# A four-layer transformer in one launch: bias, mask and weight rows change engines in four of its stages

## The chip, the cores and the metric

The kernel runs on one core of one Trainium2 chip. The metric is the time of one execution on the device, in microseconds (us); lower is better. A core has five engines that each work through a queue of their own in order: TensorE (PE, matrix products; its weight loads are PEld), VectorE (DVE), ScalarE (ACT), GpSimd (POOL) and SyncE (SP), which here only issues transfers (DMAs). An engine that needs another's result waits for a semaphore, and everything behind the waiting instruction in its queue waits with it. SBUF is the on-chip memory of 128 partitions (rows), PSUM the memory that TensorE writes its products to.

## The reference

The input x has 32 sequences of 64 tokens, 256 columns each: 2048 tokens in all. ctx_2048 is a context of the same shape. Four layers follow each other, each with a cross attention and a feed-forward part, and each part is added to x. All is float32.

```python
    x = x + _L0_xattn_ref(_layernorm(x, axis=-1), ctx_2048, ctx_2048, L0_xattn_gamma)      # stage A
    x = x + _L0_ffn_ref(_layernorm(x, axis=-1), ...)                                        # stage B
    x = x + _L1_xattn_ref(_layernorm(x, axis=-1), ctx_2048, ...)                            # stage C
    x = x + _L1_ffn_ref(_layernorm(x, axis=-1), ...)                                        # stage D
    x = x + _L2_xattn_ref(_layernorm(x, axis=-1), ctx_2048, ..., 64)                        # stage E
    x = x + _L2_ffn_ref(_layernorm(x, axis=-1), ...)                                        # stage F
    x = x + _L3_xattn_ref(_layernorm(x, axis=-1), ctx_2048, ctx_2048)                       # stage G
    x = x + _L3_ffn_ref(_layernorm(x, axis=-1), ...)                                        # stage H
```

The comments give the stage of the kernel that computes each line. What matters for the change:

- **A** is an attention over the 256 columns: 8 heads of 8 rows each, softmax over 256, for every block of 64 tokens (a sequence).
- **C** is an attention of every token over all 2048 context rows, with 16 heads of 16 columns. q, k and v are rounded to int8 steps, and the softmax weights are rounded to steps of 1/255 of the row's largest:

```python
        attn = jnp.einsum('bhqd,bhkd->bhqk', q, k)
        attn = jax.nn.softmax(attn.astype(jnp.float32), axis=-1)
        attn = _fq_unsigned(attn, axis=-1)
        out = jnp.einsum('bhqk,bhkd->bhqd', attn, v)
```

- **D** is a causal attention inside each sequence of 64 tokens (16 heads of 128 columns, with rotated q and k), followed by a mixture of 4 experts.

```python
            scores = jnp.einsum('bhqd,bhkd->bhqk', q, k) / math.sqrt(HD)
            scores = jnp.where(causal[None, None], scores, jnp.finfo(jnp.float32).min)
            probs = jax.nn.softmax(scores.astype(jnp.float32), axis=-1).astype(q.dtype)
```

- **H** is a mixture of 8 experts of 176 hidden columns, two of which count for each token, and a shared one of 352:

```python
        h = jax.nn.silu(g) * u
        eo = jnp.einsum('eni,eih->enh', h, w_down)
        combine = jnp.zeros((N, E), x.dtype).at[jnp.arange(N)[:, None], topk_i].add(topk_w)
        y = jnp.einsum('ne,enh->nh', combine, eo)
        sh = jax.nn.silu(x @ sw_gate) * (x @ sw_up)
        y = y + sh @ sw_down
```

## The kernel before, in words

**Layout.** The 2048 tokens are 16 tiles of 128 (NT = 16), which also form 4 groups of 4 tiles (NG = 4, 512 tokens). x stays in SBUF from the first load to the last store (`xs[i]`, 128 x 256 float32), and so do the context tiles. The stages run in the order A, B, C, D, E, F with G, H. The weights of a stage are loaded while the stage before it runs (`weights`, `prefetch`; the loads stand in SP's queue in the order of the program), and some stages let the start of the next one run beside their own end (the lists `heads` and `beside`).

In some stages the order of the instructions on each engine is that of the program (`manual_schedule`: A, C, E and F with G); in D and H the Tile framework's scheduler decides it from the dependencies and the pools.

**Stage A.** One tile goes through a sequence of slots (`attention_slots`). `stacked` (L195) splits the layer-normed q and the context k into three bfloat16 parts each (t3q, t3k) on GpSimd, writes the parts to a scratch in DRAM (d3q, d3k; L212) and `stack_rows` (L215) reads them back into rows 0 to 71 of two operand tiles stq and stk of 128 x 4096 bfloat16 (stq and stk are used in a ring of four). Rows 64 to 127 of these tiles are first filled with zeros (stq) and ones (stk): `operand_buffers` (L158), by VectorE, one pair of fills per ring place, for A; stage E, which uses the same functions, fills its own from two small rows by transfers. `score_maxima` takes products of the first 96 rows (L251) and the negated maximum of every row (L255, VectorE); 16 rows of these maxima are transposed, copied by ScalarE (L263 nmr, L264 nm3), split by GpSimd, and put into rows 96 to 98 of stq by transfers that ScalarE's queue issues (L271). `attend_unit` then makes the scores with the maximum taken off (L283), and the exponential (L287, ScalarE).

**Stage C** (`run_C`, L752). A step n is one tile i of queries with one head h: n = 16 i + h, 256 steps. For each step

- `scores(n, part)` (L816) makes 128 x 2048 scores in two parts of 1024. The keys kT lie two heads to a block of 128 rows. The queries qz hold one head in a 128 x 128 block of which 64 rows are zero, so that the product over 128 rows takes one head's keys alone. qz's zeros are filled once by VectorE before C (L673), and two ScalarE copies per tile (L731) put the other rows in.
- `moved(n, part)` (L844) copies a part from PSUM to SBUF on VectorE and accumulates the maximum; the second part starts from the maximum of the first (`mx[:, 0:1]`), a value that VectorE's accumulator has just written.
- `nb` (L865), on VectorE, makes the bias of the exponential from the maximum. One step's passes and its bias come in this order on VectorE: second part of n, first part of n + 1, nb of n.
- ScalarE makes `ei` (L868), the exponential as int16 with its sum, one step behind GpSimd casts it to bfloat16 (`eb`, L878), and a transposing transfer on SP's queue brings eb to eT (L880). Four steps behind, TensorE multiplies eT by the values (L829).

Beside that the queries of the next tile are made in ten portions (`queries_of_C`, L685; `next(qs)` at given heads), and the output of the tile before in seven (`output`). Both put small work on GpSimd and ScalarE between the exponentials and casts.

**Stage D** (`run_D_attention`, L1028). A unit is one head for one group of 512 tokens: 64 units. `projections` makes q and k for it (L1082), adds the bias and multiplies by the cosine on VectorE (L1084 rtq, rtk), makes shifted copies on ScalarE (L1087 rwq, rwk) and rotates on GpSimd (L1090, L1091). `scores` first writes the causal mask into PSUM by a product of the identity and a bfloat16 mask tile `causalb` (L1097), adds four 128 x 128 score products (L1100), and then works on all 512 columns at once: maximum (L1102, VectorE), subtraction (L1104, VectorE), exponential (L1105, ScalarE), sum (L1107, VectorE), reciprocal and multiplication (L1108, L1109, VectorE). The result is transposed by TensorE (L1116 sTp), multiplied by the values (L1126 op) and by the output weights (L1141 yp).

**Stage H** (`run_H`, L1809). For each of the 4 groups there are 14 chunks of 128 hidden columns: chunks 0 to 10 belong to the 8 experts laid end to end (8 x 176 = 1408 = 11 x 128), chunks 11 to 13 to the shared expert (the last has 96). A chunk is 4 gate and up products (L1844 pgate, pup), silu on ScalarE (L1852), a multiplication on VectorE (L1854 hm), and the products with the down weights into the group's output (L1820 hout), one chunk behind. For the chunks 0 to 10 each token's expert weight must be brought to the hidden columns: `routed_H` writes the weights of 512 tokens for 8 experts in three bfloat16 parts into a 96-row tile `share` (L1802 to L1806), a product of the 0/1 table `owner` with it spreads them over the chunk's 128 rows (L1848 cb), and a second multiplication puts them on (L1856). `owner` is written by three ScalarE copies at the end of stage F and G (L1760, `owners`). The chunks of a group run in the order 0 to 13.

Of the kernel before, what the change touches and what calls it, by code (L numbers as in the profile page):

```python
# [31 lines left out]
def tile_net(ctx: ExitStack, tc: tile.TileContext, a: dict, out: bass.AP):  # L32
# [119 lines left out]
    def operand_buffers(pool, k, b, row=None):  # L152

        pair = {}
        for kind, value in (("k", 1.0), ("q", 0.0)):
            pair[kind] = pool.tile([P, 16, D], BF, name=f"st{kind}{b}")
            if row is None:
                V.memset(pair[kind][64:P], value)  # L158
            else:

                nc.sync.dma_start(pair[kind][64:P], bc(row[kind][64:P], 1, [64, 16, D]))
            yield
        k.setdefault("st", []).append(pair)
# [30 lines left out]

    def stacked(pool, k, dram, src, kind, i):  # L195
# [15 lines left out]
        for t in range(n):  # L211
            nc.sync.dma_start(d3[t].rearrange("d h c -> h d c"), t3[:, t % 3, :])  # L212
        return d3

    def stack_rows(k, d3, kind, i):  # L215
        st = k["st"][i % 4][kind]
        for m in range(3):
            first = 0 if kind == "q" else m
            src = d3[first : first + 3].rearrange("t d h c -> (t d) (h c)")
            nc.sync.dma_start(st[24 * m : 24 * m + 24], src)  # L220
# [359 lines left out]
    def keys_and_values(w):  # L580
# [90 lines left out]
        w["qz"] = [qzp.tile([P, H, P], BF, name=f"qz{b}") for b in range(2)]  # L671
        for b in range(2):
            V.memset(w["qz"][b], 0.0)  # L673
# [11 lines left out]
    def queries_of_C(w, i, pool, small, psum):  # L685
# [43 lines left out]
        z = w["qz"][i % 2].rearrange("p (a b) t -> p a b t", b=2)  # L729
        for b in range(2):  # L730
            S.copy(z[64 * b : 64 * b + 64, :, b, :], tb[64 * b : 64 * b + 64])  # L731
            yield
# [19 lines left out]
    def run_C(w, side):  # L752
# [5 lines left out]
        with ExitStack() as es:  # L758
# [10 lines left out]
            with tc.tile_pool(name="C2w", bufs=1, side=side) as pool, tc.tile_pool(  # L769
# [42 lines left out]
                def scores(n, part):  # L812
                    i, h = divmod(n, H)
                    sc = psum.tile([P, 1024], F32, tag="sc", name=f"sc{part}_{n}", bufs=3)
                    for k0 in range(0, 1024, 512):
                        PE.matmul(  # L816
                            sc[:, k0 : k0 + 512], qz[i % 2][:, h, :],
                            kT[:, h // 2, 1024 * part + k0 : 1024 * part + k0 + 512], start=True, stop=True,
# [16 lines left out]
                LAG = 4  # L835
                scs, mxs, es_, eis, eTs = {}, {}, {}, {}, {}
# [17 lines left out]
                for n in range(N + LAG):  # L854
# [3 lines left out]
                    if n < N:  # L858
# [6 lines left out]
                        V.tensor_scalar(nb, mxs.pop(n)[:, 1:2], nsq[i][:, h : h + 1], LN255, ALU.mult, ALU.add)  # L865
# [23 lines left out]
                    if h in (0, 2, 3, 4, 5, 7, 8, 10, 11, 12):  # L889
# [138 lines left out]
    def run_D_attention(w, side, hs):  # L1028
# [4 lines left out]
        with ExitStack() as es:  # L1033
# [5 lines left out]
            causal = tpool.tile([P, 4, P], BF, name="causalb")  # L1039
            V.tensor_copy(causal, bc(w["causal"], 1, [P, 4, P]))  # L1040
# [53 lines left out]
            def scores(u):  # L1094
                qr, kr = qks.pop(u)
                sp = psum.tile([P, 4, P], F32, tag="sp", name="sp")
                PE.matmul(sp, identb, causal, start=True, stop=False, skip_group_check=True)  # L1097
                for j in range(4):
                    js = slice(j * P, (j + 1) * P)
                    PE.matmul(sp[:, j, :], qr[:, js], kr[:, js], start=False, stop=True, skip_group_check=True)  # L1100
                mx = pool.tile([P, 4], F32, name="mx")
                V.tensor_reduce(mx, sp, AX.X, ALU.max)  # L1102
                s = pool.tile([P, 4, P], F32, name="s", bufs=3)
                V.tensor_tensor(s, sp, bc(mx, 2, [P, 4, P]), ALU.subtract)  # L1104
                S.activation(s, s, AF.Exp, scale=scale)  # L1105
                sm = pool.tile([P, 4], F32, name="sm")
                V.tensor_reduce(sm, s, AX.X, ALU.add)  # L1107
# [178 lines left out]
    def first_of_E(w, psum):  # L1286
# [5 lines left out]
        for kind, value in (("k", 1.0), ("q", 0.0)):  # L1292
            row[kind] = cp.tile([P, D], BF, name=f"row{kind}")
# [139 lines left out]
    def run_F(w, side):  # L1433
# [12 lines left out]
        with tc.tile_pool(name="Ft", bufs=1, side=side) as tpool, tc.tile_pool(  # L1446
# [231 lines left out]
            for t in range(NT + 8):  # L1678
                for part, lag in parts:
                    if 0 <= t - lag < NT and (with_g or not part.__name__.startswith("g_")):  # L1680
                        part(t - lag)
                    if with_g and t >= NT + 1 and part.__name__ == "gained":
                        next(heads.get("owner", head), None)
# [44 lines left out]
    def load_H(wp):  # L1728
# [18 lines left out]
        owner = w["owner"] = wp.tile([96, 1408], BF, name="owner")  # L1747
        heads["owner"] = owners(owner)

        w["xnT"], w["share"] = [], []  # L1750
        for b in range(2):
            w["xnT"].append(wp.tile([P, 2, 512], F32, name=f"xnT{b}"))
            w["share"].append(wp.tile([96, 512], BF, name=f"share{b}"))
# [3 lines left out]
    def owners(owner):  # L1757
        for t in range(3):
            rows = slice(32 * t, 32 * t + 32)
            S.copy(  # L1760
# [207 lines left out]
```

## Time and profile before

| what | value |
|---|---|
| time, median of 3 runs | 2762.11 us |
| the three runs | 2757.15, 2762.11, 2770.57 us |
| the profiled execution's own time | 2769.85 us |
| its span in the profile | 2768.1 us |
| busy: PE, PEld | 2414.7 us (87%), 1431.1 us (52%) |
| busy: DVE, ACT, POOL | 1856.7 us (67%), 1532.9 us (55%), 1534.5 us (55%) |

The profiled execution is a fourth one. The stages follow each other, with some overlap at their ends, so the same engine is full in one and idle in another. Busy us by stretch of the span:

| stretch (us) | stage | PE | DVE | ACT | POOL |
|---|---|---|---|---|---|
| 0 to 300 | A | 245.6 | 225.3 | 160.9 | 167.0 |
| 300 to 508 | B, and C's keys and values | 183.4 | 111.4 | 42.6 | 84.1 |
| 508 to 1195 (687 us) | C | 519.1 | 666.1 | 613.5 | 558.1 |
| 1195 to 1820 (625 us) | D, attention | 611.2 | 341.5 | 333.3 | 342.0 |
| 1820 to 1960 (140 us) | D, experts | 137.6 | 72.0 | 57.9 | 31.9 |
| 1960 to 2270 (310 us) | E | 272.9 | 208.1 | 151.6 | 235.8 |
| 2270 to 2455 (185 us) | F and G | 135.6 | 144.6 | 124.8 | 107.6 |
| 2455 to 2768 (313 us) | H | 309.3 | 87.7 | 48.3 | 8.1 |

Busy time is the time in which an engine had an instruction in work; it says nothing by itself of what made the stage as long as it is. The ends of matrix products are modelled, so a busy TensorE is not one at its peak. A line number (L865) is that of the listing above; "nb<-mx,nsq" names the tile that an instruction writes and those that it reads.

### The profile page before, as it was taken

The page shows a single profiled execution, that of the slowest core. Times are in us where ns is not written, and L with a number is a line of the kernel's source. Part 1 is how long each engine was busy: PE and PEld are TensorE (multiplying, and loading weights), DVE is VectorE, ACT ScalarE, POOL GpSimd, SP SyncE. Part 2 cuts the span into 40 slices and gives each one's busy share as a digit, 9 for nine tenths or more (in the row PEclk, how much of TensorE's full clock was granted, in tenths as well). Part 3 has the DMA queues.
Part 4 walks back from the last instruction along what each step waited for, and adds up shares of the span by engine and source line. Part 5 has one row for each costly group of instructions (what it writes and reads, how often), then busy time and mean ns, then how long its engine had stood idle before and what let it go on. Part 6 is the DMA issues. An engine that isn't in the chain of part 4 may idle for free.

```text
span 2768.1 us, 44270 instructions
## 1 busy us (share of the span) xinstructions
PE 2414.7 (87%) x15971; PEld 1431.1 (52%) x16078; DVE 1856.7 (67%) x3913; ACT 1532.9 (55%) x2181; POOL 1534.5 (55%) x1764
## 2 busy tenths in 40 slices
PE   4999889777777777779999999999888877789999
PEld 2555344344444444436666666666555544455565
DVE  7878555799999999955454554655577758833232
ACT  1666321699999999836555555534254557731111
POOL 4565533588888888865555555513488866710000
PEclk9999999999999999989999999999999998989999
DMA  6543000599999999930000000051343311000000
GB/s 166 133 116 86 24 1 1 120 204 204 202 204 200 203 206 201 204 106 1 16 8 23 8 1 1 1 107 52 79 99 90 93 46 55 1 0 8 8 8 8
DMA packets 618919, 227.89 MB, mean 82 GB/s; under 512 B 547494, under 2 KB 608844, under 8 KB 614092
## 3 DMA queue, kind: packets, MB, share of 16 engines
q1 hardware_dynamic: 615628, 224.26, 37.1%
q8 instruction: 127, 2.08, 0.3%
q10 hardware_dynamic: 3072, 0.79, 0.2%
q14 instruction: 92, 0.75, 0.1%
HBM read 66.91 MB, written 18.87 MB: 31 GB/s over the span
## 4 chain that ended last, share of the span: by engine, by line
PE 47%; DVE 19%; issue 9%; POOL 6%; ACT 2%; DMA 1%; ACTq 0%; POOLq 0%; DVEq 0%
DVE e L844 11%; PE yp L1141 4%; PE ppq L1082 4%; PE ppk L1082 4%; PE pgate L1844 4%; PE pup L1844 4%; PE hout L1820 3%; PE vp L1070 3%; POOL e L295 2%; PE sp L1100 2%; PE op L1126 2%; PE hmp L1198 2%; PE ep L1211 2%; PE sc L816 1%; PE op L805 1%
## 5 line engine op out<-in xcount | busy, mean ns | idle before, releaser
L868 ACT ACTIVATE ei<-e,nb,sq 128x2048 int16<-128x2048 f32 x256 | 535.4, 2092 | 39.6 <-DVE nb L865 35.0
L878 POOL CAST eb<-ei 128x2048 bf16<-128x2048 int16 x256 | 482.0, 1893 | 110.7 <-ACT ei L868 92.7
L816 PE MATMUL sc<-kT,qz 128*128 128x512 bf16 x930 | 281.0, 381 | 154.6 <-DVE e L844 150.6
L255 DVE TENSOR_REDUCE negm<-s 128x2 f32<-128x512 f32 (+1 forms) x512 | 300.7, 610 | 129.1 <-PE s L251 126.3
L844 DVE TENSOR_SCALAR_CACHE_REDUCE e<-sc,mx 128x1024 f32<-128x1024 f32 x256 | 326.1, 1274 | 0.4 <-DVE nb L865 0.3
L287 ACT ACTIVATE e<-s 128x1024 f32<-128x1024 f32 (+1 forms) x256 | 233.4, 916 | 152.4 <-PE s L283 103.5
L844 DVE TENSOR_SCALAR_CACHE_REDUCE e<-sc 128x1024 f32<-128x1024 f32 x256 | 312.4, 1220 | 4.8 <-PE sc L816 4.8
L816 PEld LDWEIGHTS <-qz 128*128 128x128 bf16 x1024 | 94.6, 97 | 260.0 <-issue 202.3
L251 PE MATMUL s<-stk,stq 96*128 96x256 bf16 (+1 forms) x1024 | 192.2, 271 | 41.0 <-DMA d3k<-t3k 24.6
L1090 POOL TENSOR_TENSOR rwq<-rwq,sin 128x512 f32<-128x512 f32 x64 | 81.1, 1267 | 239.2 <-ACT rwq L1087 212.3
L283 PE MATMUL s<-stq,stk 128*128 128x256 bf16 (+1 forms) x1024 | 180.8, 262 | 11.0 <-DMA d3k<-t3k 8.4
L829 PEld LDWEIGHTS <-vz 128*64 128x64 bf16 x4096 | 122.7, 109 | 113.7 <-issue 112.7
L1854 DVE TENSOR_TENSOR hm<-pup,sl 128x512 f32<-128x512 f32 (+1 forms) x56 | 38.7, 691 | 200.2 <-PE pup L1844 197.5
L1087 ACT ACTIVATE rwq<-ppq,dbq 64x512 f32<-64x512 f32 x128 | 87.4, 683 | 153.6 <-DVE rtq L1084 150.0
L1102 DVE TENSOR_REDUCE mx<-sp 128x4 f32<-128x512 f32 x64 | 44.3, 692 | 190.8 <-PE sp L1100 190.8
L829 PE MATMUL av<-eT,vz 128*64 128x128 bf16 x4096 | 163.2, 222 | 9.3 <-DMA eT<-eb 6.8
L251 PEld LDWEIGHTS <-stq 96*128 96x128 bf16 x1024 | 94.0, 101 | 131.6 <-issue 108.7
L305 PE MATMUL o<-e,vmo 128*32 128x256 f32 (+1 forms) x2048 | 150.7, 366 | 6.2 <-POOL e L295 4.8
L295 POOL TENSOR_SCALAR_AFFINE_SELECT e<-e 128x256 f32<-128x256 f32 (+1 forms) x256 | 132.9, 546 | 30.5 <-ACT e L287 30.3
L1852 ACT ACTIVATE sl<-pgate 128x512 f32<-128x512 f32 (+1 forms) x56 | 33.4, 597 | 207.9 <-PE pgate L1844 207.8
L91 POOL TENSOR_TENSOR rstd<-ve,mhalf 128x1 f32<-128x1 f32 (+1 forms) x40 | 25.9, 646 | 185.3 <-DVE ve L89 83.7
L1070 PE MATMUL vp<-Dwv,hnT 128*128 128x512 f32 x256 | 122.2, 600 | 6.1 <-ACT hnT L949 5.5
(406 smaller groups left out, 5443.1 us busy)
## 6 DMA issues: line engine op xcount, KB each, us to landing
stk<-d3k SPq DMA_DIRECT2D x96, 192.0 KB
stq<-d3q SPq DMA_DIRECT2D x96, 192.0 KB
d3k<-t3k SPq DMA_DIRECT2D x160, 64.0 KB
d3q<-t3q SPq DMA_DIRECT2D x96, 64.0 KB
eT<-eb SPq DMA_TRANSPOSE x256
fw<-in_L_ffn_w SPq DMA_DIRECT2D x3, 1024.0 KB
x<-in_x SPq DMA_DIRECT2D x16, 128.0 KB
c<-in_ctx SPq DMA_DIRECT2D x16, 128.0 KB
```

The lines of the kernel that those rows point to most:

```text
L251: PE.matmul(sc[:, hh, lo:hi], qs[0:96, 2 * hp + hh, qc * P : (qc + 1) * P], ks[0:96, 2 * hp + hh, lo:hi], start=band is None, stop=True, s ...
L255: V.tensor_reduce(negm[:, qc, 2 * hp : 2 * hp + 2], sc[:, :, lo:hi], AX.X, ALU.max, negate=True)
L287: S.activation(e[:, :, lo:hi], sc[:, :, lo:hi], AF.Exp, scale=scale)
L295: G.affine_select(e[:, :, s0:s1], e[:, :, s0:s1], [[0, 4], [step, s1 - s0]], ALU.is_ge, 0.0, base=base, channel_multiplier=chan,)
L816: PE.matmul(sc[:, k0 : k0 + 512], qz[i % 2][:, h, :], kT[:, h // 2, 1024 * part + k0 : 1024 * part + k0 + 512], start=True, stop=True,)
L829: PE.matmul(av[i][r0 : r0 + 64, h // 4, :], vz[:, kt, h // 4, h % 4, :], eT[:, kt, :], start=h == 0 and kt < 2, stop=h == H - 1 and kt >= ...
L844: V.tensor_scalar(e, scs.pop((n, part)), 1.0, mx[:, 0:1] if part else LOWEST, ALU.mult, ALU.max, accum_out=mx[:, part : part + 1],)
L868: S.activation(ei, es_.pop(n), AF.Exp, bias=nb, scale=sq[i][:, h : h + 1], accum_out=sums[i][:, h : h + 1],)
L878: G.tensor_copy(eb, eis.pop(n - 1))
L1070: PE.matmul(vp, hnT[g][:, c, j * P : (j + 1) * P], wv[:, c, :], start=c == 0, stop=c == 1)
L1082: PE.matmul(pp, wt[:, c, hh * P : (hh + 1) * P], hnT[g][:, c, :], start=c == 0, stop=c == 1)
L1844: PE.matmul(pp[:m], w[nm + "s"][:, c, cols], xnT[:, c, :], start=c == 0, stop=c == 1)
```

## The change

It has four parts that do not touch each other.

1. **Stage A.** The first fills of the operand tiles are made by ScalarE, as a multiplication of a broadcast row of ones by 1 or 0. The first tile's q transfers (d3q and the rows of stq) are issued by ScalarE's queue in place of SP's. Stage E keeps SP.
2. **Stage C.** qz loses its zero rows and is half as large: the score products take the 64 rows of their head from it and from kT. Its fills are gone, and one copy per tile takes the place of two. nb is made by GpSimd for nine of the 16 heads (3, 4, 5, 7, 8, 11, 12, 14, 15) and stays on VectorE for the others. The queries of the next tile are advanced in nine portions instead of ten.
3. **Stage D.** The mask product and `causalb` are gone. VectorE adds the mask while it moves the scores to SBUF, takes the maximum from there and multiplies it by the negated scale. Four exponentials of 128 columns, each with its own bias and its own sum as an accumulator, take the place of the subtraction, the one exponential and the sum.
4. **Stage H.** `owner`, `share` and the cb products are gone. `routed_H` writes the 8 x 512 weights to a scratch in DRAM, and for every routed chunk one or two broadcasting transfers on SP's queue (18 per group) bring the rows to a tile wc of 128 x 512, three chunks ahead. The second multiplication takes wc from SBUF. The shared chunks come first: 11, 12, 13, then 0 to 10.

```diff
 def operand_buffers(pool, k, b, row=None):
-                V.memset(pair[kind][64:P], value)
+                dst = pair[kind][64:P].rearrange("p h (a c) -> p (h a) c", c=P)
+                S.mul(dst, bc(ones[64:P], 1, [64, 32, P]), value)
...
+    def queue_of(k, kind, i):
+        return nc.scalar if kind == "q" and i == 0 and "row" not in k else nc.sync
...
-            nc.sync.dma_start(d3[t].rearrange("d h c -> h d c"), t3[:, t % 3, :])
+            queue_of(k, kind, i).dma_start(d3[t].rearrange("d h c -> h d c"), t3[:, t % 3, :])
...
-            nc.sync.dma_start(st[24 * m : 24 * m + 24], src)
+            queue_of(k, kind, i).dma_start(st[24 * m : 24 * m + 24], src)
```

```diff
-        w["qz"] = [qzp.tile([P, H, P], BF, name=f"qz{b}") for b in range(2)]
-        for b in range(2):
-            V.memset(w["qz"][b], 0.0)
+        w["qz"] = [qzp.tile([P, H // 2, P], BF, name=f"qz{b}") for b in range(2)]
...
-        z = w["qz"][i % 2].rearrange("p (a b) t -> p a b t", b=2)
-        for b in range(2):
-            S.copy(z[64 * b : 64 * b + 64, :, b, :], tb[64 * b : 64 * b + 64])
-            yield
+        S.copy(w["qz"][i % 2], tb)
+        yield
...
+                    rows = slice(64 * (h % 2), 64 * (h % 2) + 64)
...
-                            sc[:, k0 : k0 + 512], qz[i % 2][:, h, :],
-                            kT[:, h // 2, 1024 * part + k0 : 1024 * part + k0 + 512], start=True, stop=True,
+                            sc[:, k0 : k0 + 512], qz[i % 2][rows, h // 2, :],
+                            kT[rows, h // 2, 1024 * part + k0 : 1024 * part + k0 + 512], start=True, stop=True,
...
+                BUSY = (0, 1, 2, 6, 9, 10, 13)
...
-                        V.tensor_scalar(nb, mxs.pop(n)[:, 1:2], nsq[i][:, h : h + 1], LN255, ALU.mult, ALU.add)
+                        (V if h in BUSY else G).tensor_scalar(nb, mxs.pop(n)[:, 1:2], nsq[i][:, h : h + 1], LN255, ALU.mult, ALU.add)
...
-                    if h in (0, 2, 3, 4, 5, 7, 8, 10, 11, 12):
+                    if h in (0, 2, 3, 4, 5, 7, 8, 10, 11):
                         next(qs, None)
```

```diff
-                PE.matmul(sp, identb, causal, start=True, stop=False, skip_group_check=True)
                 for j in range(4):
                     js = slice(j * P, (j + 1) * P)
-                    PE.matmul(sp[:, j, :], qr[:, js], kr[:, js], start=False, stop=True, skip_group_check=True)
+                    PE.matmul(sp[:, j, :], qr[:, js], kr[:, js], start=True, stop=True)
+                s = pool.tile([P, 4, P], F32, name="s", bufs=3)
+                V.tensor_tensor(s, sp, bc(w["causal"], 1, [P, 4, P]), ALU.add)
                 mx = pool.tile([P, 4], F32, name="mx")
-                V.tensor_reduce(mx, sp, AX.X, ALU.max)
-                s = pool.tile([P, 4, P], F32, name="s", bufs=3)
-                V.tensor_tensor(s, sp, bc(mx, 2, [P, 4, P]), ALU.subtract)
-                S.activation(s, s, AF.Exp, scale=scale)
+                V.tensor_reduce(mx, s, AX.X, ALU.max)
+                V.tensor_scalar(mx, mx, -scale, None, ALU.mult)
                 sm = pool.tile([P, 4], F32, name="sm")
-                V.tensor_reduce(sm, s, AX.X, ALU.add)
+                for j in range(4):
+                    S.activation(
+                        s[:, j, :], s[:, j, :], AF.Exp, bias=mx[:, j : j + 1], scale=scale, accum_out=sm[:, j : j + 1]
+                    )
```

```diff
-        S.copy(sh[0:8], src)
-        V.tensor_tensor(r, src, sh[0:8], ALU.subtract)
-        G.tensor_copy(t, r)
-        G.tensor_copy(sh[32:40], t)
-        G.tensor_tensor(sh[64:72], r, t, ALU.subtract)
+        sh = pool.tile([8, 512], F32, name="sh")
+        S.copy(sh, tp[0:8].rearrange("e j t -> e (j t)"))
+        w["shares"][g] = w["dram"].tile([8, 512], F32, name="shd")
+        nc.sync.dma_start(w["shares"][g], sh)
...
+            ORDER = [11, 12, 13] + list(range(11))
+            def weights_of(n):
+                g, ch = divmod(n, 14)
+                ch = ORDER[ch]
+                if ch < 11:
+                    wc = wcs[n] = pool.tile([P, 512], F32, name="wc", bufs=4)
+                    e, r0 = ch * P // 176, 0
+                    while r0 < P:
+                        r1 = min(P, 176 * (e + 1) - ch * P)
+                        nc.sync.dma_start(wc[r0:r1], w["shares"][g][e : e + 1, :].to_broadcast([r1 - r0, 512]))
+                        e, r0 = e + 1, r1
...
-                    if ch < 11:
-                        cb = psum.tile([P, 512], F32, tag="cb", name="cb")
-                        PE.matmul(cb, owner[:, cols], sh, start=True, stop=True)
+                if n + 3 < 14 * NG:
+                    weights_of(n + 3)
...
-                    if ch < 11:
-                        V.tensor_tensor(hm, hm, cb, ALU.mult)
+                if n in wcs:
+                    V.tensor_tensor(hm, hm, wcs.pop(n), ALU.mult)
```

With these the loops of run_H over g and ch become one over n = 14 g + k, and the order of the program changes the place of some weight loads on SP's queue: stage D's expert weights come later and its first attention weights (Dwq, Dwk, Dwo) earlier.

## The prediction

> **What bounds the kernel now.** I read the table of busy time by stage first, because the shares of the whole span mix stages with different limits. Its columns after the stretch and its length are PE, PEld, DVE, ACT and POOL busy time with counts, granted TensorE clock, share of the DMA engines and GB/s.
>
> ```profile
> 550.00:1150.00 600.00, 460.82 (x5004) 254.03 (x5090) 594.34 (x1194) 548.61 (x574) 500.86 (x343) 1.00 1.01 203
> 1270.00:1760.00 490.00, 489.37 (x2163) 326.00 (x2164) 251.79 (x430) 266.93 (x430) 265.80 (x212) 1.00 0.03 8
> 2455.00:2768.00 313.00, 309.28 (x1023) 182.06 (x1021) 87.72 (x178) 48.34 (x75) 8.08 (x10) 0.99 0.02 7
> ```
>
> Row one is stage C, the all-token attention: VectorE is busy 99%, and whatever it does not lose is worth nothing. Row two is stage D's attention and row three stage H: TensorE is busy 99.9% and 98.8%, so what leaves TensorE there leaves the time. The DMA share of 1.01 in row one looks like a bound and is not: the single packets show one 524 KB transpose served in 1.8 us, then idle engines, in a step of 2.56 us.
>
> Second, the groups by line (busy us, mean ns of one) for the two operations that meet on GpSimd, and VectorE's timeline in stage C.
>
> ```profile
> L878 POOL CAST eb<-ei 128x2048 bf16<-128x2048 int16 x256 | 482.0, 1893 | 110.7 <-ACT ei L868 92.7 <-DMA eT<-eb 16.1 <-ACT qz L731 1.6
> L865 DVE TENSOR_SCALAR nb<-mx,nsq 128x1 f32<-128x1 f32 x256 | 53.5, 209 | 0.0
> ```
>
> ```profile
> 803.36 0.21 DVE L865 TENSOR_SCALAR nb<-mx,nsq 128x1 f32<-128x1 f32 x1
> 803.57 1.28 DVE L844 TENSOR_SCALAR_CACHE_REDUCE e<-sc,mx 128x1024 f32<-128x1024 f32 x1
> 804.77 0.08 DVE L844 DVE_READ_ACCUMULATOR e<-sc,mx 128x1 f32 x1
> ...
> 814.03 0.21 DVE L865 TENSOR_SCALAR nb<-mx,nsq 128x1 f32<-128x1 f32 x1
> 814.15 0.24 DVE L784 RECIPROCAL rs<-sums 128x16 f32<-128x16 f32 x1
> 814.31 1.20 DVE L844 TENSOR_SCALAR_CACHE_REDUCE e<-sc,mx 128x1024 f32<-128x1024 f32 x1
> 815.44 0.08 DVE L844 DVE_READ_ACCUMULATOR e<-sc,mx 128x1 f32 x1
> ```
>
> The reader is to see that the step with the bias alone takes 804.77 - 803.36 = 1.41 us from one accumulator read to the next, and the step with the bias and a reciprocal also 815.44 - 814.03 = 1.41. The extra 0.24 us instruction was free, so VectorE's own work does not fill this gap.
>
> Third, TensorE in stage D and stage H.
>
> ```profile
> 1438.79 0.38 PE L1097 MATMUL sp<-causalb,identb 128*128 128x512 bf16 x1
> 1439.00 1.05 PE L1100 MATMUL sp<-rtk,rtq 128*128 128x128 f32 x8
> ```
>
> ```profile
> 2463.63 1.73 PE hout L1820 x8
> 2469.01 1.73 PE hout L1820 x8
> ```
>
> ```profile
> 2752.07 1.88 PE L1844 MATMUL pgate<-xnT,hwgate 128*128 128x512 f32 x4
> 2757.23 1.88 PE L1844 MATMUL pgate<-xnT,hwgate 128*96 128x512 f32 x4
> ```
>
> The causal product holds TensorE for 1439.00 - 1438.79 = 0.21 us (its printed 0.38 is latency). A routed chunk of H, which has the cb product, takes 2469.01 - 2463.63 = 5.38 us; a shared one, which has not, 2757.23 - 2752.07 = 5.16. Last, the start of stage A.
>
> ```profile
> 24.64 1.01 PE L251 MATMUL s<-stk,stq 96*128 96x256 bf16 x4 [24.64 <-DMA d3k<-t3k]
> 26.87 3.47 DVE L158 MEMSET stk<- 64x4096 bf16 x1 [0.91 <-issue]
> 33.25 1.18 PE L251 MATMUL s<-stk,stq 96*128 96x256 bf16 x4 [6.66 <-DVE negm L255]
> ```
>
> VectorE's fill of a later tile's operands stands in front of the maxima that free TensorE's buffers: 6.66 us of idle TensorE here, 6.61 us again at 51.68.
>
> **The change part by part.**
>
> *Stage C, bias to GpSimd in 9 of 16 heads.* It removes 9 x 16 = 144 instructions of 0.209 us from VectorE. What is late next is the following pass (e<-sc,mx), which takes its starting maximum from the accumulator read just before. In the trace's semaphore records that read, begun at 803.362, raises its count at 803.456; the next pass's wait passes at 803.483, and an instruction on an otherwise idle VectorE starts 0.065 us after its wait passes (median of 153). So without the bias it would start at 803.548 instead of 803.565: 0.017 us. Bounds: nothing, or a small loss if GpSimd is late, and the full 0.209. I take 0.017, as the reciprocal above says the same: 144 x 0.017 = **-2.4 us**. The Trainium skill speaks otherwise ("VectorE: DVE Perf Modes", The DRAIN you can't avoid, and Rules for kernel authors): a semaphore between chained VectorE instructions cost nothing extra, so one should lower the count of instructions, not of semaphores. By that rule 144 x 0.209 = -30 us. The row decides.
>
> GpSimd takes the 144 instructions on: the nearest rows are its two small multiplies, 0.27 (L710) and 0.20 us (L712). Each stands before the cast of the step before, and that cast, its transpose on SP's queue and the product wait behind it. GpSimd is busy 500.86 of 600, or 34.8 us of a tile's 41.7, so 6.9 us are free and 9 x about 0.3 = 2.7 fit. ScalarE gains: GpSimd's bias needs only the second maximum, which is ready a full pass (1.14 us) before VectorE gets to its own. The seven heads that stay on VectorE hold or follow GpSimd's other work (x sums, scale, rounding, avs).
>
> *Scores over 64 rows, one qz copy.* Same 512 columns per product; TensorE idles 139 of 600 us, so nothing. One copy of 128x1024 for two of 64x1024 (1.0 us each): ScalarE loses 16 us of busy time, cover as before, nothing. The two qz fills (0.91 us at 461.2 and 466.8) stood in VectorE's idle time in stage B: nothing.
>
> *Stage D, causal mask by VectorE.* 64 products of 0.21 us leave the bound engine: **-13.6 us**. VectorE per unit: out go the sum reduce (0.69) and nothing else of size (maximum stays, the subtraction becomes the mask's addition, both 0.69), in comes a 128x4 scaling of about 0.2: less than now. ScalarE: one Exp of 0.63 becomes four of 128 columns with bias and accumulator. Nearest rows: the 128x256 Identity with accumulator, 0.41 us start to start; less 128 columns x 0.84 ns, plus about 0.1 for the pointer: 0.40 each, 1.6 together, +1.0 per unit. ScalarE is busy 5.1 of 9.3 us per unit, so it fits. Chain: -0.69 + 0.2 + 1.0 = +0.5 us, then the rotation's reads of q (rtq) wait 0.5 us longer behind it, and ScalarE's shifted copies behind those. Cover: s is ready at 1434.5 and transposed at 1438.35, 3.8 us later. Were that gone, each unit would give back the whole 0.21. The instruction order on every engine is otherwise the same. Weight loads change places on SP's queue (expert weights later, the first Dwq, Dwk, Dwo earlier); they are wanted late, nothing.
>
> *Stage H, weights' rows by transfers.* 44 cb products leave: 44 x 0.22 = **-9.7 us**. In come per group 18 broadcast reads and one 16 KB write on SP's queue, three chunks (over 15 us) ahead of use; only the output stores stand behind them. The nearest row is bkv in stage A's tail, the same 128x512 broadcast: issued at 301.91, and its packets, with 512 KB more, are through by 305.3. 3.4 us fit in 5.16. The shared chunks come first, so the first group's rows have time; the last chunk now has a second multiply (0.69 us), which the previous chunk's products (1.73 us) cover but for 0.1. Three owner copies of 1.36 us leave ScalarE at the end of F/G, mostly beside other waits: **-0.5 us**.
>
> *Stage A, first fills by ScalarE.* VectorE loses 5.2 us of fills per tile for four tiles. At the start that frees the second tile's statistics (10.71, after fills), whose GpSimd step stood in front of the first tile's t3q: that comes 4 us earlier, and TensorE starts at about 21.5. Now the Trainium skill against it: "ScalarE: Activation LUTs", Rules for kernel authors, says multiplies belong on VectorE, per element faster there. Rows: 128x1024 Exp 1.023 and 128x768 0.809 us give 0.84 ns per column, so 4096 columns cost 1.02 + 3072 x 0.84 ns = 3.6 us, a pair 7.2 against 5.2. By the rule alone this part is a loss of 2 us per tile; by the trace it pays, as ScalarE is idle until 41.40. It is not free: q's first transfers, now on ScalarE's queue, wait between fills, and the fourth tile's pair (7.2 us) stands before the copies of the first maxima (L263, L264). These would come at about 42.5 instead of 44.26, the first scores at 48 instead of 57.5. But tile 2's operands then bind: SP issues them only after stage B's weights, whose last (sdown) waits until 46.82 now; some 5 us earlier in the new order, so they land at 54 where slot 32 is reached at 59.7 today. I take the smaller: **-5.5 us**; bounds -10 (both idle gaps) and +2.
>
> Sum: -2.4 - 13.6 - 9.7 - 0.5 - 5.5 = -31.7 us. The profiled execution took 2769.85 us (span 2768.1): 2738.2 after. It lies 7.7 above the median of the runs shown, 2762.11, so on their scale 2730.4.
>
> **The rivals.** (1) The bias's time comes off in full, -30 instead of -2.4: 2703. For it: the rule, and VectorE at 99%. Against: the free reciprocal. (2) Stage D keeps its pace, because four Exps and the later rtq make ScalarE or VectorE late: -18.1, so 2744. For it: longer chain. Against: 3.8 us of slack. (3) Slower: GpSimd becomes stage C's bound. A bias waits for its maximum at the head of GpSimd's queue while a ready cast stands behind it. It decides from 6.9 / 9 = 0.77 us of GpSimd per bias; at 1.1 us, about one VectorE pass, it costs 9 x 0.33 x 16 = 48 us: 2762.1 - 29.3 + 48 = 2781. For it: one queue, 1.89 us casts in a 2.56 us step. Against: rows of 0.2 to 0.27 us and the earlier maximum. (4) H's rows arrive late or the start gains nothing while something unseen takes the rest: about 2755.
>
> **How the numbers follow.** The main case has 0.66 and lies between 2718 and 2742 by its bounds; (1) 0.10, (2) 0.06, (3) 0.12, (4) 0.06. The three runs span 0.5%, which is about what can be told from no change here: faster by more than that is below 2748. Main, (1) and (2) are faster: 0.82, less 0.02 for their tails: 0.80. Same 0.07, slower 0.13. The range takes in (1), at 2703, and (2), at 2744, with some us of margin for the run: 2700 to 2751.
>
> **What would show it.** Right: stage C's tiles stay within 0.3 us of 41.7; D's unit falls from 9.31 to 9.10; H's routed chunk to 5.17, with no idle time by wc; TensorE's waits of 6.6 us at the start are gone and the first scores come before 54. Wrong: C's tile at 40.0 (rival 1), above 42.5 with ei waiting on GpSimd's nb (rival 3), D's unit at 9.3 (rival 2).

## The result: slower, and the profile after

| what | before | after |
|---|---|---|
| time, median | 2763.26 us (4 runs, 2757.15 to 2770.57) | 2913.74 us (4 runs, 2906.11 to 2916.89) |
| ratio after / before | | 1.0539, 95% interval 1.0506 to 1.0573 |
| span of the profiled execution | 2768.1 us | 2914.1 us |
| mean granted TensorE clock | 0.977 | 0.857 |

The forecast was 2730. From the first and last instructions of each stage in the two traces, the spans' difference of +145.9 us comes apart so:

| stretch | after - before | forecast |
|---|---|---|
| start to stage C's first pass (A, B, C's keys) | -4.9 | -5.5 |
| C, first pass to last exponential | **+172.9** (670.0 to 842.9) | -2.4 |
| end of C to end of D's experts | -9.6 | -13.6 |
| E, F and G | -2.8 | -0.5 |
| H | -9.7 | -9.7 |

Outside stage C every part moved the way that was forecast, D by less. The -2.8 us of E, F and G can't be told from chance: in the seven traces without these changes their length runs from 490.4 to 493.5 us, and it is 490.8 here. The row PEclk of the page after (the granted clock in tenths, in 40 slices of 73 us) says what happened in C:

```profile
PE   5999898999999999998899999999988896879999
PEclk9999999555566555656999999999999998989999
```

The labels take five places; the eighth to the nineteenth slice, which are stage C, have a clock of 5 to 6 tenths, and TensorE is busy nearly throughout in them. The table by stretch after, for C, D's attention and H (columns as before: after the length PE, PEld, DVE, ACT and POOL busy with counts, clock, DMA share, GB/s):

```profile
500.00:1340.00 840.00, 812.61 (x5526) 396.50 (x5525) 660.03 (x1181) 586.94 (x612) 588.18 (x515) 0.58 0.76 160
1620.00:1920.00 300.00, 300.00 (x1321) 198.68 (x1320) 154.78 (x273) 198.49 (x494) 166.32 (x132) 1.00 0.02 8
2611.00:2912.00 301.00, 299.23 (x979) 177.77 (x977) 86.04 (x174) 48.32 (x75) 0.89 (x1) 0.99 0.14 42
```

In C the bound has moved: VectorE, 99% busy before, has 660 of 840 us (79%), TensorE 813 of 840 (97%), at a clock of 0.58. Of the waits from 520 to 1340 us, with the engine that waits, what it waits for, the us in total, the times and the longest:

```profile
DVE e L848 <- PE sc L819: 162.6, 175, 5.0
ACT ops L809 <- PE op L807: 95.1, 14, 6.8
```

TensorE's timeline shows one step in each state of the clock, and what separates them:

```profile
653.98 1.89 PE L819 MATMUL sc<-kT,qz 64*128 64x512 bf16 x4
655.79 1.07 PE L832 MATMUL av<-eT,vz 128*64 128x128 bf16 x16
656.79 1.88 PE L819 MATMUL sc<-kT,qz 64*128 64x512 bf16 x4
...
660.75 3.78 PE L807 MATMUL op<-wp,avs 128*128 128x256 f32 x8
...
666.28 1.06 PE L819 MATMUL sc<-kT,qz 64*128 64x512 bf16 x4
667.28 0.64 PE L832 MATMUL av<-eT,vz 128*64 128x128 bf16 x16
```

At 653.98 a step takes TensorE 656.79 - 653.98 = 2.81 us, more than the 2.56 us that VectorE needs. The four score products are 1.81 us of it, against 667.28 - 666.28 = 1.00 us after the output product (op), a burst of float32 products over all 128 rows; behind it the clock's records show 1.00 for 6.8 us, and 0.50 for 47.8 us before. The median step of the trace is 2.81 us where a step has nothing else on TensorE; where the queries' and the output's products come in, which lay in TensorE's idle time before, they now stand in series: the step with the output product takes 7.62 us instead of 2.99. A tile takes 53.2 us instead of 41.8.

### The profile page after: what moved, and what is told of

It is laid out like the page before. It is cut to its first block, busy times and chain, and to the rows that moved or that the text cites. A ratio compares the mean times of both kernels' runs of the same rounds, so it can differ in the third digit from the quotient of the medians.

```text
span 2914.1 us, 44768 instructions
## 1 busy us (share of the span) xinstructions
PE 2698.1 (93%) x15960; PEld 1536.1 (53%) x15970; DVE 1821.9 (63%) x3754; ACT 1605.3 (55%) x2618; POOL 1563.4 (54%) x1894
## 4 chain that ended last, share of the span: by engine, by line
PE 64%; DVE 9%; POOL 5%; issue 3%; ACT 2%; DMA 1%; ACTq 0%; DVEq 0%; POOLq 0%
PE sc L819 13%; PE av L832 7%; PE yp L1146 4%; PE ppq L1085 3%; PE ppk L1085 3%; PE pgate L1843 3%; PE hout L1819 3%; PE pup L1843 3%; PE vp L1073 3%; DVE e L848 3%; PE sp L1102 2%; PE op L1131 2%; PE op L807 2%; PE hmp L1203 2%; PE ep L1216 2%
## 5 line engine op out<-in xcount | busy, mean ns | idle before, releaser
L819 PE MATMUL sc<-kT,qz 64*128 64x512 bf16 x1024 | 439.0, 568 | 27.4 <-DVE e L848 26.2
L832 PEld LDWEIGHTS <-vz 128*64 128x64 bf16 x4096 | 191.6, 155 | 189.8 <-issue 189.8
L832 PE MATMUL av<-eT,vz 128*64 128x128 bf16 x4096 | 247.9, 294 | 3.2 <-DMA eT<-eb 3.2
L819 PEld LDWEIGHTS <-qz 64*128 64x128 bf16 x1024 | 101.9, 119 | 215.9 <-issue 204.0
L1104 DVE TENSOR_TENSOR s<-sp,causal 128x512 f32<-128x512 f32 x64 | 44.2, 691 | 165.9 <-PE sp L1102 165.9
L1110 ACT ACTIVATE s<-s,mx 128x128 f32<-128x128 f32 x256 | 99.6, 390 | 81.0 <-DVE mx L1107 79.7
```

The lines of the kernel that those rows point to most:

```text
L819: PE.matmul(sc[:, k0 : k0 + 512], qz[i % 2][rows, h // 2, :], kT[rows, h // 2, 1024 * part + k0 : 1024 * part + k0 + 512], start=True, sto ...
L832: PE.matmul(av[i][r0 : r0 + 64, h // 4, :], vz[:, kt, h // 4, h % 4, :], eT[:, kt, :], start=h == 0 and kt < 2, stop=h == H - 1 and kt >= ...
```

## The experiments

Theory 1: products over 64 rows let the clock fall, and TensorE becomes C's bound. Theory 2: the bias on GpSimd holds C up, and the low clock follows from TensorE's gaps. Times of one comparison share their runs of the kernel before.

**Full rows again in the changed kernel.** The cut shows the products alone; qz's zero rows with their fills, the second copy and the tenth portion of the queries come back with them.

```diff
-                            sc[:, k0 : k0 + 512], qz[i % 2][rows, h // 2, :],
-                            kT[rows, h // 2, 1024 * part + k0 : 1024 * part + k0 + 512], start=True, stop=True,
+                            sc[:, k0 : k0 + 512], qz[i % 2][:, h, :],
+                            kT[:, h // 2, 1024 * part + k0 : 1024 * part + k0 + 512], start=True, stop=True,
```

> The changed kernel with stage C's score products over 128 rows again (qz with its zero rows, two copies); the bias stays on GpSimd in nine heads, and A, D and H stay as changed. Theory 1 (rows): products over 64 rows let TensorE's granted clock fall to 0.5, and TensorE then bounds stage C; here the clock is 1.00 in C again, C takes about 670 us from its first maximum to its last exponential instead of 843, and the time is 2913.7 - 173 = about 2740. Theory 2 (bias): the bias on GpSimd holds the exponentials up, TensorE gets its work late and the clock falls for lack of work; here the time stays at about 2910 and the clock at about 0.58 in C.

Measured: 2744.85 us, ratio to before 0.9925 (0.991 to 0.994); C takes 674.0 us. The clock of C, from 550 to 1150 us, is the third figure from the end:

```profile
550.00:1150.00 600.00, 458.81 (x4967) 253.03 (x5053) 578.19 (x1058) 544.27 (x572) 531.67 (x470) 1.00 1.01 202
```

The whole loss goes with this edit, which the next run narrows down.

**64 rows alone, in the kernel before.**

```diff
-                            sc[:, k0 : k0 + 512], qz[i % 2][:, h, :],
-                            kT[:, h // 2, 1024 * part + k0 : 1024 * part + k0 + 512], start=True, stop=True,
+                            sc[:, k0 : k0 + 512], qz[i % 2][rows, h, :],
+                            kT[rows, h // 2, 1024 * part + k0 : 1024 * part + k0 + 512], start=True, stop=True,
```

> The kernel before with nothing changed but the score products, which take their head's 64 rows of qz and kT. Theory 1 (rows): clock about 0.58 in stage C and 2763 + 173 = about 2936. Theory 2 (bias): nothing changes, 2763 and clock 1.00.

Measured: 2939.89 us, ratio 1.0632 (1.0612 to 1.0651).

```profile
550.00:1150.00 600.00, 584.70 (x3957) 287.83 (x3953) 471.33 (x927) 430.14 (x445) 393.30 (x267) 0.57 0.77 158
```

Theory 2 has fallen, and theory 1 holds: which rows two operands are read from costs 174 us, with every other instruction the same. C's tile takes 53.3 us here with all biases on VectorE, as in the changed kernel: once TensorE is the bound, the bias makes no difference.

**What does the clock follow?** The next runs change rows and columns in use by known shares.

64 rows in the second part of the scores alone (`rows = ... if part else slice(0, P)`):

> The kernel before with 64 rows in the second part of the scores of every step alone, 128 in the first. A step of 2.56 us has 4 score products of 512 columns and 16 value products of 128, each half 0.85 us at full clock; weighted by the rows in use, TensorE works 67% of the step in the kernel before, 50% with 64 rows throughout, 58% here. Theory 1 with a threshold: the clock is either near 1.00 and the time 2763, or it falls as with 64 rows throughout and the time lies above 2880; a time of half the loss (2850) speaks for a loss in proportion instead of a threshold. Theory 2 (bias): 2763.

Measured: 2786.38 us, ratio 1.0073 (1.0047 to 1.0098). Neither figure of the threshold came out. The records of the clock show why: it is 1.00 or 0.50, never between, but it changes some thirty times in C, in low stretches of 3.4, 6.8, 10.2 or 13.7 us. The mean over 550 to 1150 us is 0.93.

64 rows throughout, value products 128 columns wide:

```diff
-                            av[i][r0 : r0 + 64, h // 4, :], vz[:, kt, h // 4, h % 4, :], eT[:, kt, :],
+                            av[i][:, h // 4, :], vz[:, kt, h // 4, c0 : c0 + 2, :].rearrange("p c m -> p (c m)"), eT[:, kt, :],
```

> The kernel before with 64 rows in all score products, and with value products 128 columns wide instead of 64 (they take two heads' values at once, so the sums of the heads are mixed in the output). What does the clock gate count? If rows in use: 50% of the step as with 64 rows throughout, so the clock stays at about 0.58 in stage C and the time at about 2936. If cells (rows times columns) in use: 0.5 x 0.85 + 0.85 = 1.28 of 2.56 us, 50%, as in the kernel before (0.85 + 0.5 x 0.85), against 33% with 64 rows and narrow value products; then the clock is 1.00 and the time 2763.

Measured: 2780.28 us in two executions, ratio 1.0052 (1.0032 to 1.0072). Clock 1.00 from 550 us on, after a first 41 us of C at 0.50. By its own count the expectation says cells. The next run was to confirm that.

Full rows, value products 32 columns wide:

```diff
-                            av[i][r0 : r0 + 64, h // 4, :], vz[:, kt, h // 4, h % 4, :], eT[:, kt, :],
+                            av[i][r0 : r0 + 32, h // 4, :], vz[:, kt, h // 4, h % 4, c0 : c0 + 32], eT[:, kt, :],
```

> The kernel before with its scores over 128 rows, and with value products 32 columns wide instead of 64 (the 32 that hold the head's values; the others are zero in the kernel before). Rows in use stay at 67% of the step; cells in use fall from 50% to (0.85 + 0.25 x 0.85) / 2.56 = 42%, which is what 64 rows in half of the scores gave. If the clock gate counts cells, C's clock is near the 0.92 of that run and the time near its 2786; if it counts rows or busy time, the clock is 1.00 and the time 2766.

Measured: 2763.52 us, ratio 0.9996 (0.9987 to 1.0005).

```profile
550.00:1150.00 600.00, 457.74 (x5004) 247.71 (x5090) 594.57 (x1194) 548.06 (x575) 500.24 (x344) 1.00 1.02 203
```

That is not what cells predict, so the two runs contradicted each other by my count. The count was wrong: single instructions in the traces show neighbouring 64-column value products starting 3 and 53 ns apart in turn. They go to different halves of the columns and run side by side, so 16 of them take 0.43 us of array time and not 0.85; the 128-column ones start 56 ns apart. Two runs followed with that counted.

The 16 value products in the order 0, 2, ... 14, 1, 3, ... 15, and 64 rows throughout:

```diff
-                    for kt in range(NT):
+                    for kt in [*range(0, NT, 2), *range(1, NT, 2)]:
```

> The kernel before with 64 rows in all score products, and with the 16 value products of a step in another order: first the eight that go to one half of the columns, then the eight of the other. In the kernel before two neighbours go to the two halves and run side by side (starts 3 and 53 ns apart in turn), so the 16 take 0.43 us of array time and not the 0.85 that the earlier expectations counted; the 128-column products stood 56 ns apart, one by one. Counted so, rows in use are 50% of a step in the kernel before, 33% with 64 rows throughout, 42% with 64 rows in half of the scores, and 50% in both runs that changed the value products; cells in use are 50, 33, 42, 50 and 42%. Here the new order should put the value products one behind the other: rows in use (0.43 + 0.85) / 2.56 = 50%, cells 33%, as in the slow kernel with 64 rows. Theory rows: clock 1.00 in C but for its start, and 2763 to 2780. Theory cells: clock 0.58 and about 2940.

Measured: 2846.26 us, ratio 1.0298 (1.0273 to 1.0323), between both figures. The order did less than intended: around the change from one half to the other the starts are still 25 to 30 ns apart, so the value products take about 0.72 us, which makes 45% of rows in use, not 50%. And the clock was low in 137 of C's first 156 us, and 0.91 to 0.94 from 760 to 1120 us:

```profile
520.00:640.00 120.00, 116.78 (x704) 61.80 (x702) 88.90 (x177) 82.12 (x85) 74.21 (x50) 0.57 0.73 157
760.00:880.00 120.00, 107.19 (x962) 61.16 (x961) 113.02 (x228) 104.11 (x112) 92.99 (x65) 0.94 0.93 190
```

64 rows in one of the four score products of a step:

> The kernel before with 64 rows in one of the four score products of a step. Rows in use: (0.875 x 0.85 + 0.43) / 2.56 = 46%, between the 50% that hold the clock and the 42% of 64 rows in half of the scores, whose clock fell for 107 of 690 us of stage C and which cost 20 us. If the edge lies below 46%, the clock is 1.00 and the time 2763; if it is softer, some us of the 20 are lost here too.

Measured: 2768.77 us, ratio 1.0016 (1.0007 to 1.0026), so there is no sharp edge in this count: C spends 32 us at 0.50 here and 9 in the kernel before. All of them, counted alike (share of a 2.56 us step at full clock, side-by-side products once), with the mean clock from 550 to 1150 us and the time:

| scores / values | rows in use | cells in use | clock | us |
|---|---|---|---|---|
| 128 rows / 64 columns (before) | 50% | 50% | 1.00 | 2763 |
| 128 rows / 32 columns | 50% | 42% | 1.00 | 2763.5 |
| 64 rows / 128 columns | 50% | 50% | 1.00 | 2780.3 |
| a quarter over 64 rows / 64 columns | 46% | 46% | 0.99 | 2768.8 |
| 64 rows / 64 columns, other order | 45% | 33% | 0.84 | 2846.3 |
| half over 64 rows / 64 columns | 42% | 42% | 0.93 | 2786.4 |
| 64 rows / 64 columns | 33% | 33% | 0.57 | 2939.9 |

Cells alone are excluded by the pairs with 33% (0.84 against 0.57) and with 42% (1.00 against 0.93). Rows in use order all but one pair: 45% came out below 42%, most of it in the first 156 us of C.

**The same traces, window by window.** The clock's changes lie multiples of 3.41 us apart, so stage C of each trace can be cut into the windows that they mark. Let each product count with its time at full clock (0.216 us for 512 columns of bfloat16, as the starts show, and twice that for a float32 record) times the share of the 128 rows that it uses, side-by-side products once, as a share of the window. The changed kernel around the output product at 660.75 us:

| window from (us) | 654.8 | 658.3 | 661.7 | 665.1 | 668.5 | 671.9 |
|---|---|---|---|---|---|---|
| rows in use in it | 29% | 25% | 44% | 50% | 34% | 24% |
| clock in it | 0.50 | 0.50 | 0.50 | 1.00 | 1.00 | 0.50 |

The clock follows one window later. One level, 37%, tells the clock of the next window in all but 24 of the 2484 windows of the twelve traces, and it is the same level for falling and for returning. Of these windows 566 are followed by 0.50, so that calling every one 1.00 would miss 566. With the best level for each, TensorE's busy time misses 552, the time under products of all 128 rows 136, and cells 94. The level was fitted to these windows of stage C; in the 7119 others that the clock's records cover it misses 46. The count is an estimate: products that a trace lacks (94 of 1024 scores in the kernel before) were put in from their weight loads.

This also accounts for the pair out of order. At half clock the same work takes longer, so it is a smaller share of a window. A step of scores and values takes 2.81 us there with 64 rows, 3.64 with the wide values, 3.24 with the other order; the 33%, 50% and 45% of the table become 30%, 35% and 36%. So the kernel with wide values, low at C's start, stayed low at 34% of a window until the transposes of the next queries made one of 39%. The other order falls about as often as half of the scores over 64 rows (13 and 16 low stretches), but 13 of its 71 windows at half clock reach 37%, against 13 of 28.

**The bias, with full rows.** On VectorE in all heads (`V.tensor_scalar(nb, ...)`), with A, D and H as changed:

> The changed kernel with 128-row scores and with the bias on VectorE in all 16 heads, so stage C is that of the kernel before and A, D and H stay as changed. With 128-row scores and the bias on GpSimd in nine heads C took 674.0 us from its first maximum to its last exponential, against 670.0 in the kernel before. If the bias on GpSimd costs these 4 us, C is back at 670 and the time at 2744.9 - 4 = 2741. If the prediction's gain of 2.4 us for the bias holds and the 4 us are of another origin, C gets longer, 676, and the time is 2747.

Measured: 2738.0 us, ratio 0.9903 (0.9886 to 0.992); C takes 669.7 us.

On GpSimd in all heads (`G.tensor_scalar(nb, ...)`):

> The changed kernel with 128-row scores and the bias on GpSimd in all 16 heads. GpSimd's bias took 0.26 us here. If each bias costs on average what it did with nine (4.0 / 144 = 0.028 us), C takes 670 + 7 = 677 us and the time is 2748. If the seven heads left out are those where GpSimd is late (its work for the next tile's queries), C takes over 685 us and the time is over 2756. By rival 3 of the prediction it is bound from 6.9 / 16 = 0.43 us per bias, so GpSimd's busy time alone would not be the bound.

Measured: 2754.09 us, ratio 0.9968 (0.9955 to 0.9981); C takes 686.0 us. So the bias on GpSimd costs 4.3 us of C in nine heads and 16.3 in sixteen; the seven heads left out are the dear ones. With sixteen the times show the loss as well. With nine their intervals overlap, and the sign rests on stage C: 674.0 us in one trace, against 669.5 to 670.0 in the four with full rows and all biases on VectorE. VectorE's timeline of the kernel with nine shows that the instruction itself was free:

```profile
784.74 0.09 DVE L851 DVE_READ_ACCUMULATOR e<-sc 128x1 f32 x1
784.74 0.21 DVE L873 TENSOR_SCALAR nb<-mx,nsq 128x1 f32<-128x1 f32 x1
784.95 1.28 DVE L851 TENSOR_SCALAR_CACHE_REDUCE e<-sc,mx 128x1024 f32<-128x1024 f32 x1
...
787.30 0.08 DVE L851 DVE_READ_ACCUMULATOR e<-sc 128x1 f32 x1
787.51 1.28 DVE L851 TENSOR_SCALAR_CACHE_REDUCE e<-sc,mx 128x1024 f32<-128x1024 f32 x1
...
789.86 0.08 DVE L851 DVE_READ_ACCUMULATOR e<-sc 128x1 f32 x1
...
813.84 0.42 DVE L712 TENSOR_REDUCE amq<-qps 128x16 f32<-128x256 f32 x1 [0.44 <-ACT qq L709]
```

With the bias on VectorE the pass starts 784.95 - 784.74 = 0.21 us after the accumulator's read; without it 787.51 - 787.30 = 0.21 us, idle. The step is 2.56 us both ways. With nine heads the loss is in one step of a tile (5.1 us over the stage, some of it given back in others), where VectorE's maximum of the next queries (amq) waits for ScalarE's copy (qq), 0.44 us in this one: this step has a median of 2.84 us with all biases on VectorE, 3.22 with nine on GpSimd and 3.67 with sixteen. With sixteen the last step of a tile (head 15) adds 5.4 us, which is not explained. That the exponential ahead of the copy, itself held by a bias on GpSimd, makes the copy late is how I read the waits; no run changed it alone.

**A version that beats both.** Full rows, all biases on VectorE, A, D and H as changed, and stage B's weights requested later:

```diff
-                if i == 3:
+                if i == 8:
                     pending.pop()()
```

> Candidate for the best version: 128-row scores, all biases on VectorE, A, D and H as changed, and stage B's weights requested at stage A's tile 8 instead of tile 3. In the changed kernel SyncE's queue holds the third tile's operands behind these loads, the last of which it issues 5.7 us late (43.62 us, the one before ended at 37.91), and TensorE waits 4.0 us for the operands at 55.03. If that wait is on the path, the time is 4 us under that of the same kernel without this edit, 2737; if the pace of the later tiles makes the wait good, the same 2741.

Measured: 2736.58 us, ratio 0.9899 (0.9884 to 0.9914), against 2738.0 in the same comparison without this edit. The wait of 4.0 us is gone from TensorE's timeline, but the times can't be told apart: the later tiles' pace makes it good, or nearly. Either version is some 25 us faster than the kernel before.

## Why the prediction was wrong

**The step that failed** is "Same 512 columns per product; TensorE idles 139 of 600 us, so nothing." It priced the half-height products by their columns, at the clock that the row of before showed, and took that clock for a constant. The clock is an answer to the load. With 64 rows a step uses 33% of the array's rows over time instead of 50%, below the 37% at which it fell in these traces; at half clock TensorE then needs 2.81 us for a step of which VectorE needs 2.56. The cost put at nothing is 2939.9 - 2766.3 = 174 us for this edit alone. None of the rivals had it; the slower one named GpSimd, whose bias took 0.26 us in the runs, far below its 0.77. The Trainium skill ("TensorE: Matmul & The Clock Gate", Part 1, What's actually happening) says that the clock depends on how busy TensorE has been, judged in windows of about 3.4 us, and is either half or full. The two states and the 3.4 us grain are what these traces show. That a busy TensorE keeps its clock is not: here it was 97% busy at half of it. By a rule of busy time alone this edit would have left the kernel at 2766 us, as I had it; it took 2939.9.

**The bias.** The free instruction was read rightly: the forecast of 0.017 us per step against the rule's 0.209 stands, and the measured step is equal to 0.01 us. The sign of the term was wrong, +4.3 against -2.4, for a wait elsewhere that the prediction held to fit: it checked GpSimd's free time and not who is queued behind the exponentials on ScalarE.

**Stage D.** The unit fell from 9.31 to 9.10 us, as the starts of the output products (yp) before and of the transposes (sTp) after show:

```profile
1318.98 1.73 PE yp L1141 x8
1328.30 1.73 PE yp L1141 x8
1337.61 1.73 PE yp L1141 x8
```

```profile
1651.24 0.60 PE L1121 MATMUL sTp<-ident,s 128*128 128x128 f32 x4
1660.35 0.60 PE L1121 MATMUL sTp<-ident,s 128*128 128x128 f32 x4
1669.44 0.60 PE L1121 MATMUL sTp<-ident,s 128*128 128x128 f32 x4
```

The mis-sized term is the count of 64. With full rows again the last 55 intervals gained 9.8 us, but the first eight units lost 2.3, so from the first value product to the last output product D gained 7.5 and not 13.6 (8.1 in the changed kernel itself). At the start nothing covers the chain: TensorE's wait for the first softmax is 6.30 us instead of 5.56, the half microsecond that the prediction had added to the chain and then hidden. In the later units the chain is a whole microsecond longer (the softmax is ready 2.8 us before its transposes, 3.8 before the change) and still covered. The rest of the 2.3 is not explained. A low clock at D's start is hardly part of it: two traces without the change and one with it (that of sixteen heads) have the same low stretches from the first value product on, and the eight units still differ by 2.0 us.

**Stage H.** -9.7 us forecast, -9.7 measured; routed chunks are 5.16 us, and no wait names the transfers of wc.

```profile
2664.20 1.88 PE L1843 MATMUL pgate<-xnT,hwgate 128*128 128x512 f32 x4
2669.36 1.88 PE L1843 MATMUL pgate<-xnT,hwgate 128*128 128x512 f32 x4
```

**Stage A.** The first scores came at 46.75 us (48 forecast, 57.5 before), and the third tile's operands then held TensorE until 55.03 (54 forecast). The first scores before, and both lines after:

```profile
57.53 0.63 PE L283 MATMUL s<-stq,stk 128*128 128x256 bf16 x2
```

```profile
46.75 0.61 PE L289 MATMUL s<-stq,stk 128*128 128x256 bf16 x2 [3.20 <-DMA stq<-nm]
55.03 0.61 PE L257 MATMUL s<-stk,stq 96*128 96x256 bf16 x2 [4.03 <-DMA d3k<-t3k]
```

A's last product (den) ends at 289.5 us in the mean of the four traces with this part (286.5 to 291.9) and at 293.6 in the seven without (290.7 to 296.3): -4.1 where -5.5 was forecast. One trace of each would not have told it. A, D and H together gave 24.9 us with the bias on VectorE in all heads (2762.9 to 2738.0), of the 29.3 forecast.

## What to carry to other kernels

A TensorE that idles is no proof that its work is free to change shape: products that use half of the rows do half the work in the same time, and in these runs the clock was granted by that work. Before narrowing a product, look at the granted clock of the stage and at what else fills the array there; the zeros that a full-height product multiplies may be what keeps the stage at full speed. And when an instruction moves to another queue, free time on that queue is not enough: follow the chain through the next engine to whoever waits at its end.

## What the runs showed of the hardware

- The granted clock followed rows in use rather than busy time: 1.00 at 50% of a step, 0.99 at 46%, 0.93 at 42%, 0.57 at 33%, with TensorE busy 584.7 of 600 us in the last; 0.84 at 45% where the work was spread over more time at half clock. It takes only the values 1.00 and 0.50, in stretches that are multiples of 3.4 us.
- Window by window, the clock went to 1.00 or stayed there behind a stretch of 3.41 us with 37% of the rows in use or more, and to 0.50 behind one with less, in all but 70 of 9603 windows (an estimate from the twelve traces).
- Rows full of zeros in one operand count as used: qz's zero half, loaded as weights, kept the clock at 1.00.
- A low clock can hold itself: with 64-row scores and wide values a step used 50% at full clock, which stayed at 1.00, and 35% at half clock, which stayed at 0.50 for C's first 41 us.
- Two 64-column products to different halves of the columns run side by side, 3 ns apart, so 16 of them cost what 8 would.
